# A four-layer graph attention kernel: groups of three row tiles in place of four, and a bias as three bf16 rows

## The chip, the cores and the metric

The kernel runs on one core of a Trainium2 chip. The metric is the device time of one execution in microseconds. The engines are named as in the profile: PE (TensorE, with PEld for its weight loads), DVE (VectorE), ACT (ScalarE), POOL (GpSimd) and SP, whose queue issues most DMAs.

## The reference

Four graph attention layers run over 4096 nodes with 256 features. Each ends in a residual sum and a layer norm. The adjacency matrix has density 1/256 plus the diagonal, about 17 neighbours a row, and all layers share it.

```python
# x (4096, 256) f32, adj (4096, 4096) int32
x = layernorm(x + L0(x, adj))     # 4 heads of 64: e = leaky(s_i + d_j, 0.2), masked softmax over j, times h
x = layernorm(x + L1(x, adj))     # 4 heads of 64, the same form
x = layernorm(x + L2(x, adj))     # 2 heads of 128, with biases b1, b2 (scores) and b3 (values)
x = layernorm(x + L3(x, adj))     # 1 head: softmax(e) @ x and -softmax(-e) @ x, joined, times fc_W, elu
```

## The kernel before

Rows are handled in 32 row tiles of 128 nodes. In `Program.run`, a layer is a sequence of row tiles (`Layer.steps`), each in two halves, and each row tile that is finished is projected for the next layer (`Projection`: transpose, two matmuls against the weights, factors, a store of the values row to DRAM).

There are two ways to compute a row tile. A *gathered* tile (`RowTile`) knows by a list which neighbours its rows have; the list is built during layer 0. It loads its own rows of values by a DMA on SP (L792) and the neighbours' by 13 indirect DMAs on POOL (L797), six for the first half and seven for the second. `RowTile.half` then forms the weights: ACT's Exp (L907; in layer 3 L874 to L877), DVE's mask (L864, L909, L876, L878), and PE multiplies weights and gathered values (L928). The units of a half are of two kinds: those of `FULL` use 128 columns of weights, those of `PAIRS` use 64 columns twice. The own rows are unit 0, the only one of `FULL[0]`.

An *all-node* tile is computed against all 4096 nodes instead. `WHOLE` lists, for each layer, blocks of four such row tiles (`BT = 4`); `ORDER` holds the rest, which are gathered. `whole_heads` does a block in layer 1 and `whole_rows` in layers 2 and 3. Both are generators: each `yield` ends one unit, the work of one block of 128 neighbours for all four row tiles of the block. A unit loads one `vw` tile of values (SP), spreads the bits of the adjacency to bytes (`bytes`, L660), forms the weights of 128 x 512 elements (DVE's L1275 in layer 1, with a product of exponentials and a maximum; ACT's L1200 or L1203 to L1207 and DVE's L1201 or L1208 in layers 2 and 3) and multiplies (PE: L1278 and L1280 in layer 1, L1211 in layers 2 and 3). A block has 64 units in layer 1 (two turns of two heads), 32 in layer 2 and 64 in layer 3 (two signs).

`half_with_whole` writes the order of a half step down: transposes of tiles to be projected, the half of the gathered tile, copies and matmuls of the projections, the end of the previous tile, then a share of the units. The share is set by `whole`:

```python
while self.between is None and self.used < self.total \
        and self.used < self.ahead + (self.total - self.ahead) * (step + 1) / (2 * self.count - 6):
    self.unit()
```

So the units are spread evenly over the half steps of the layer and end three tiles before it does. Ten units of the next layer (`AHEAD`) run at the change of layers, in `close`. A scheduler then places the instructions of each engine, so the final order can differ from the written one by a little.

The bias of layer 2 is added in `Projection.multiply`: a matmul of a column of ones with one row `brow` of 262 float32 numbers, after the two matmuls of the projection (L691, then L694). `weights(2)` builds that row.

`norm` collects finished rows and normalises them in groups; `GROUPS` gives the size of a group up to a tile number. `MIX = 23`: first halves gather only from tiles 0 to 22, second halves from all.

Of the kernel before, what the change touches and what calls it, by code (L numbers as in the profile page):

```python
# [81 lines left out]
GROUPS = (((24, 4),), ((24, 2), (28, 1), (31, 2)), ((16, 2), (17, 1), (20, 2), (24, 1), (31, 2)), ((24, 1), (31, 4)))  # L82
# [32 lines left out]
WHOLE = ((), (1, 7), (3, 7, 6), (7, 6))  # L115
AHEAD = 10
ORDER = tuple([m for m in range(NT) if m // BT not in w] for w in WHOLE)
# [66 lines left out]
class Program:  # L184
# [27 lines left out]
    def weights(self, n):  # L212
# [5 lines left out]
        if n < 2:  # L218
            nc.sync.dma_start(out=wext[:, :, :F], in_=to_tiles(ins[f"W{n}T"]))
            for k, a in enumerate(("src", "dst")):  # L220
                ablk = self.small.tile([P, KT, H4], F32, name=f"ablk{k}")
                nc.vector.memset(ablk, 0.0)
                for h in range(H4):
                    r = slice((h % 2) * D4, (h % 2) * D4 + D4)
                    vec = ins["a0s" if k == 0 else "a0d"][h] if n == 0 else ins["a1"][h, k * D4:(k + 1) * D4]
                    load_vec(nc, ablk[r, h // 2, h:h + 1], vec)
                ablks.append(ablk)
                nats.append(ins[f"W{n}"])
        elif n == 2:
            nc.sync.dma_start(out=wext[:, :, :F], in_=to_tiles(ins["W23T"]))  # L230
            for k in range(2):
                ablk = self.small.tile([P, KT, 2], F32, name=f"ablk{k}")
                nc.vector.memset(ablk, 0.0)
                for h in range(2):
                    load_vec(nc, ablk[:, h, h:h + 1], ins["a2"][h, k * P:(k + 1) * P])
                ablks.append(ablk)
                nats.append(ins["W21" if k == 0 else "W22"])
            brow = self.small.tile([1, F + 3 * H], F32, name="brow")
            nc.sync.dma_start(out=brow[:, :F], in_=ins["b23"].rearrange("(o f) -> o f", o=1))
            ones = self.small.tile([1, P], F32, name="ones")  # L240
            nc.vector.memset(ones, 1.0)
            self.ones = ones
        else:
            fc = to_tiles(ins["fc3"])
            for k in range(2):
                nc.sync.dma_start(out=wext[:, :, k * F:(k + 1) * F], in_=fc[:, k * KT:(k + 1) * KT, :])
                ablk = self.small.tile([P, KT, 1], F32, name=f"ablk{k}")
                for q in range(KT):
                    load_vec(nc, ablk[:, q, 0:1], ins["a3"][(k * KT + q) * P:(k * KT + q + 1) * P])
                ablks.append(ablk)  # L250
                nats.append(ins["W3T"])
# [29 lines left out]
        return wext, brow  # L281


    def lists(self, ctx):
# [94 lines left out]
        class Block:  # L379
# [21 lines left out]
            def squeeze(self, part):  # L401
# [10 lines left out]
                if part == BT - 1:  # L412
                    rows = shared["v"][0][self.blk % 2][:N, :BW].rearrange("(j p) w -> p j w", p=P)
                    nc.sync.dma_start(out=rows, in_=self.bits.rearrange("p j t w -> p j (t w)").bitcast(F32))
                    if any(self.blk in w for w in WHOLE):
                        nc.sync.dma_start(out=shared["bitsW"][self.blk], in_=self.bits)
# [189 lines left out]
    def run(self):  # L606
        ins, nc = self.ins, self.nc
        nothing = self.small.tile([1, max(PITCH)], F32, name="nothing")
# [148 lines left out]
class RowTile:  # L757
# [77 lines left out]
    def half(self, half):  # L835
# [82 lines left out]
        for t, heads in enumerate(turns):  # L918
            for us in (FULL[half], PAIRS[half])[::-1 if t == 1 and (half == 1 or n < 3) else 1]:
                for h in heads:  # L920
                    for u in us:
                        for rows, g in parts[u]:
                            a = accs[h][rows, :Wd] if n == 3 else accs[0][rows, h * Wd:(h + 1) * Wd]
                            b = g[:, h * Wd:(h + 1) * Wd]
                            if n < 2:
                                a = accs[0][rows, h * Wd:(H + 1) * Wd].rearrange("p (s c) -> p s c", c=Wd)[:, ::H - h]
                                b = b.rearrange("p (s c) -> p s c", s=1).to_broadcast([P, 2, Wd])
                            nc.tensor.matmul(a, w[h][:, u, rows], b,  # L928
                                             start=half == 0 and u == 0 and (n == 3 or h == turns[0][0]),
                                             stop=half == 1, skip_group_check=True)  # L930
# [24 lines left out]
class Layer:  # L955
# [3 lines left out]
    def __init__(self, prog, n):  # L959
# [6 lines left out]
        self.total = len(WHOLE[n]) * ((NT if n == 2 else 2 * NT) + (BT if n < 2 else 0))  # L966
# [201 lines left out]
    def whole_rows(self):  # L1168
# [3 lines left out]
        for blk in WHOLE[n]:  # L1172
            tiles = range(blk * BT, (blk + 1) * BT)
# [3 lines left out]
            bits = self.block_bits(blk)  # L1177
            zs = [None] * BT
            for heads in groups:
                accs = [prog.bank(prog.pfour) for _ in range(BT)]  # L1180
# [11 lines left out]
                for j in range(NT):  # L1192
# [3 lines left out]
                    for h in heads:  # L1196
                        p = prog.dp.tile([P, BT, P], F32, name="pw")
                        d = sh["d"][n][:, j, h if n < 3 else 0:h + 1 if n < 3 else 1]
                        if n < 3:
                            nc.scalar.activation(p, S[:, h], AF.Exp, bias=d)  # L1200
                            nc.vector.scalar_tensor_tensor(p, p, LEAST, mj, op0=ALU.max, op1=ALU.mult)  # L1201
                        else:
                            nc.scalar.activation(p, S[:, 0], AF.Relu, bias=d)  # L1203
# [6 lines left out]
                        for it in range(BT):  # L1210
# [3 lines left out]
                    if n == 3 and heads[0] == 0 and j == NT - 1:  # L1214
                        def between(accs=accs):
                            for it in range(BT):
                                zs[it], last = self.positive(accs[it], whole=True)
                            return last
# [8 lines left out]
    def whole_heads(self):  # L1227
# [8 lines left out]
        def scores(blk):  # L1236
            S = prog.bk.tile([P, T, BT, P], F32, name="Sw", bufs=2)
            for it in range(BT):
                nc.sync.dma_start(out=S[:, :, it, :], in_=sh["e"][n][blk * BT + it].partition_broadcast(P))
            return S  # L1240
# [11 lines left out]
        for q, blk in enumerate(WHOLE[n]):  # L1252
            tiles, S = range(blk * BT, (blk + 1) * BT), later
            bits = self.block_bits(blk)
            z = prog.bk.tile([P, BT, H, Wd], F32, name="zh")
            for up, flat in TWOS:
# [11 lines left out]
                for j in range(NT):  # L1268
# [4 lines left out]
                    for h in (up, flat):  # L1273
                        p[h] = prog.dp.tile([P, BT, P], F32, name="pw")
                        nc.vector.scalar_tensor_tensor(p[h], S[:, h], c[:, j, h:h + 1], mj, op0=ALU.max, op1=ALU.mult)  # L1275
                    how = dict(stop=j == NT - 1, skip_group_check=True)
                    for it in range(BT):
# [10 lines left out]
                nc.scalar.copy(z[:, :, up, :], bu[:, :BT * Wd].rearrange("p (t c) -> p t c", t=BT))  # L1288
                turned = prog.bk.tile([Wd, BT, P], F32, name="turned")
                nc.scalar.copy(turned, bf[:Wd, :].rearrange("p (t i) -> p t i", t=BT))  # L1290
                self.set_banks()
                bt = prog.bank(prog.banks)
                for it in range(BT):
                    nc.tensor.transpose(bt[:, it * Wd:(it + 1) * Wd], turned[:, it, :], sh["ident"][:Wd, :Wd])
                nc.scalar.copy(z[:, :, flat, :], bt[:, :BT * Wd].rearrange("p (t c) -> p t c", t=BT))
            y = self.load_x(tiles[0])
            for it, m in enumerate(tiles):
                yield
                self.finish(m, z[:, it].rearrange("p h c -> p (h c)"), y, None)
                if it + 1 < BT:  # L1300
                    y = self.load_x(m + 1)

    def block_bits(self, blk):
        bits = self.prog.mwp.tile([P, NT, BT, MW], I32, name="bw")
        self.nc.sync.dma_start(out=bits, in_=self.shared["bitsW"][blk])
        return bits

    def bytes(self, bits, j):
        mj = self.prog.mup.tile([P, BT, P // 4], I32, name="mw")
        spread(self.nc, mj, bits[:, j], self.shared["pat"])  # L1310
        return mj.rearrange("p t i -> p (t i)").bitcast(U8).rearrange("p (t i) -> p t i", t=BT)
# [548 lines left out]
```

## Time and profile before

| | us |
|---|---|
| median of 5 runs | 2786.59 |
| lowest and highest | 2770.5, 2790.01 |
| the profiled execution | 2783.01 |
| its span, first to last instruction | 2781.2 |
| mean granted TensorE clock | 0.834 |

| busy in the span | us | share | instructions |
|---|---|---|---|
| PE | 2126.6 | 76% | 15865 |
| DVE | 1597.4 | 57% | 5138 |
| ACT | 1553.4 | 56% | 4806 |
| POOL | 1319.3 | 47% | 1335 |

A matmul of float32 shows as two records. The busy time of a group is the union of its rows; the mean duration of one is longer than the distance between two starts, since matmuls overlap in the array. Layer 0, with the building of the lists, takes about the first 1100 us; layers 1, 2 and 3 take the rest in nearly equal parts. The DMA queues moved 454.91 MB.

### The profile page before, as it was taken

To read this page: it belongs to the slowest core of one execution; us is meant where nothing else is said; L and a number is where in the kernel's file an instruction comes from. 1 tells how busy PE (TensorE), PEld (TensorE's weight loads), DVE (VectorE), ACT (ScalarE), POOL (GpSimd) and SP (SyncE) were. 2 spreads that over 40 slices of the span, in tenths; PEclk is the share of its full clock that TensorE was granted. 3 is DMA by queue.
4 is the path that set the end of the run, shared out by engine and by line. 5 is a ranking of instruction groups with operands and counts; after the bars stand their busy time and mean duration, and the time that the engine had idled before them with its cause. 6 is when DMAs were issued, how large, how long until landed. Compare 5 with 4: busy or idle time off the path is not lost. (4 is left out here: it accounts for less than half of the span.)

```text
span 2781.2 us, 48223 instructions
## 1 busy us (share of the span) xinstructions
PE 2126.6 (76%) x15865; PEld 1714.2 (62%) x15865; DVE 1597.4 (57%) x5138; ACT 1553.4 (56%) x4806; POOL 1319.3 (47%) x1335
## 2 busy tenths in 40 slices
PE   5636766666667768588888887758899888999997
PEld 3335545544545556477777786647787766676675
DVE  3335535554553446466666776536777574667675
ACT  5436545554554345555555555546766656666674
POOL 0244443444444343644444453355666426666663
PEclk7657767776776779799989998868999899999998
DMA  8757555554543345444444443335556557778774
GB/s 276 252 184 231 165 159 169 160 169 156 169 150 99 91 142 145 114 122 130 124 131 126 131 137 112 107 98 146 161 166 165 136 162 217 232 238 250 240 237 142
DMA packets 299344, 454.91 MB, mean 164 GB/s; under 512 B 89830, under 2 KB 215371, under 8 KB 299084
## 3 DMA queue, kind: packets, MB, share of 16 engines
q0 software_dynamic: 72384, 220.69, 27.4%
q1 hardware_dynamic: 222082, 226.84, 27.3%
q10 hardware_dynamic: 4618, 4.20, 0.4%
q8 instruction: 128, 2.10, 0.3%
q14 instruction: 132, 1.08, 0.1%
HBM read 402.49 MB, written 49.08 MB: 162 GB/s over the span
## 5 line engine op out<-in xcount | busy, mean ns | idle before, releaser
L797 POOL DMA_INDIRECT G<-vals,idx x1300 | 1313.8, 1011 | 1432.5 <-issue 582.0
L928 PE MATMUL bank<-G,w 128*64 128x130 f32 (+5 forms) x8708 | 1089.6, 332 | 371.8 <-issue 333.6
L928 PEld LDWEIGHTS bank<-G,w 128*64 128x64 f32 (+1 forms) x8708 | 840.6, 175 | 598.2 <-issue 499.9
L907 ACT ACTIVATE w<-S,G 128x64 f32<-128x64 f32 (+1 forms) x3248 | 864.8, 351 | 191.4 <-PE bank L928 70.2
L1211 PE MATMUL bank<-vw,pw 128*128 128x129 f32 (+1 forms) x2560 | 439.5, 327 | 47.1 <-issue 38.7
L1211 PEld LDWEIGHTS bank<-vw,pw 128*128 128x128 f32 x2560 | 386.0, 198 | 96.3 <-issue 57.3
L864 DVE SCALAR_TENSOR_TENSOR w<-w,bank 128x1024 f32<-128x1024 f32 (+1 forms) x224 | 299.4, 1346 | 58.5 <-ACT w L907 39.0
L1275 DVE SCALAR_TENSOR_TENSOR pw<-Sw,cw,mw 128x512 f32<-128x512 f32 x256 | 185.1, 747 | 114.1 <-remote 62.9
L691 PE MATMUL bank<-wext,xT 128*128 128x268 f32 (+3 forms) x640 | 198.9, 446 | 28.1 <-ACT xT L682 15.0
L1200 ACT ACTIVATE pw<-Sw,d 128x512 f32<-128x512 f32 x192 | 135.1, 713 | 128.8 <-remote 86.1
L1280 PE MATMUL bank<-pw,vw 128*65 128x128 f32 x1024 | 198.1, 279 | 4.2 <-issue 4.2
L1201 DVE SCALAR_TENSOR_TENSOR pw<-pw,mw 128x512 f32<-128x512 f32 x192 | 130.3, 687 | 117.7 <-ACT pw L1200 78.9
L1278 PE MATMUL bank<-vw,pw 128*128 128x65 f32 x1024 | 175.4, 256 | 7.7 <-issue 6.0
L1278 PEld LDWEIGHTS bank<-vw,pw 128*128 128x128 f32 x1024 | 157.9, 196 | 15.0 <-issue 11.6
L691 PEld LDWEIGHTS bank<-wext,xT 128*128 128x128 f32 x640 | 129.2, 218 | 59.2 <-ACT xT L682 18.6
L742 ACT ACTIVATE erow<-bank,shift 4x128 f32<-4x128 f32 (+1 forms) x96 | 34.0, 354 | 208.1 <-PE bank L732 114.0
L874 ACT ACTIVATE w<-S,G 128x64 f32<-128x64 f32 (+1 forms) x329 | 105.3, 352 | 79.6 <-DMA G<-vals,idx 44.6
L399 ACT ACTIVATE mk<-raw 128x1024 uint8<-128x1024 int32 x128 | 129.2, 1049 | 22.2 <-DMA raw<-in_adjB_dram 12.8
L711 ACT ACTIVATE row<-bank 128x4 f32<-128x4 f32 (+1 forms) x128 | 21.5, 168 | 206.4 <-remote 109.4
L1208 DVE TENSOR_TENSOR pw<-pw,mw 128x512 f32<-128x512 f32 x128 | 87.8, 689 | 82.5 <-issue 27.4
L682 ACT COPY xT<-bank 128x256 f32<-128x256 f32 x128 | 45.9, 362 | 130.3 <-PE bank L677 67.3
L1203 ACT ACTIVATE pw<-Sw,d 128x512 f32<-128x512 f32 x128 | 90.0, 710 | 45.3 <-remote 20.4
(195 smaller groups left out, 2055.5 us busy)
## 6 DMA issues: line engine op xcount, KB each, us to landing
raw<-in_adjB_dram SPq DMA_DIRECT2D x128, 512.0 KB
G<-vals,idx POOLq DMA_INDIRECT x1300
vw<-vals SPq DMA_DIRECT2D x128, 130.0 KB
vw<-vals SPq DMA_DIRECT2D x128, 128.5 KB
S<-edge SPq DMA_DIRECT2D x56, 256.0 KB
vw<-vals SPq DMA_DIRECT2D x96, 129.0 KB
xp<-y SPq DMA_DIRECT2D x96, 128.0 KB
y<-xp SPq DMA_DIRECT2D x96, 128.0 KB
```

The lines of the kernel that those rows point to most:

```text
L399: nc.scalar.activation(self.mk[:, 2 * q:2 * q + 2], src, AF.Copy)
L691: nc.tensor.matmul(pp[:, :c1 - c0], self.xT[:, k, :], wext[:, k, c0:c1], start=(k == 0), stop=(k == KT - 1 and brow is None))
L797: nc.gpsimd.indirect_dma_start(out=self.row(half, k), out_offset=None, in_=self.values[:N + 1 if half else MIX * P, :].rearrange("r (k c) ...
L864: return nc.vector.scalar_tensor_tensor(pair, pair, LEAST, mh2, op0=ALU.max, op1=ALU.mult)
L907: nc.scalar.activation(w[h][:, u, rows], S[:, h, rows], AF.Exp, bias=d(g, h))
L928: nc.tensor.matmul(a, w[h][:, u, rows], b, start=half == 0 and u == 0 and (n == 3 or h == turns[0][0]), stop=half == 1, skip_group_check=True)
L1200: nc.scalar.activation(p, S[:, h], AF.Exp, bias=d)
L1201: nc.vector.scalar_tensor_tensor(p, p, LEAST, mj, op0=ALU.max, op1=ALU.mult)
L1211: nc.tensor.matmul(accs[it][:, c:c + Wd], p[:, it, :], v[:, c:c + Wd], start=(j == 0 and h == heads[0]), stop=(j == NT - 1), skip_group_ch ...
L1275: nc.vector.scalar_tensor_tensor(p[h], S[:, h], c[:, j, h:h + 1], mj, op0=ALU.max, op1=ALU.mult)
L1278: nc.tensor.matmul(bu[:, it * Wd:(it + 1) * Wd], p[up][:, it, :], v[:, up * Wd:(up + 1) * Wd], start=j == 0 and it == 0, **how)
L1280: nc.tensor.matmul(bf[:Wd, it * P:(it + 1) * P], v[:, flat * Wd:(flat + 1) * Wd], p[flat][:, it, :], start=j == 0 and it == 0, **how)
```

## The change

It has four parts.

- `WHOLE` now holds ranges of row tiles instead of block numbers. Layer 1 has tiles 5-7 and 29-31 where it had 4-7 and 28-31; layer 2 has 12-15, 28-31 and 25-27 where it had 24-27; layer 3 has 28-31 and 25-27 where it had 24-27. So two more row tiles are gathered in layer 1, one more in layer 2 and one more in layer 3, and the loops of `whole_heads` and `whole_rows` run over `g = len(tiles)`. The number of units is as before (128, 96 and 128); a unit of a group of three has weights of 128 x 384 and three quarters of the matmuls. `GROUPS` is moved by a tile to fit.
- In layer 3, the first half of a gathered tile multiplies its own rows for both signs before the neighbours' for both; before it did own and neighbours' rows of one sign, then those of the other.
- The bias row of layer 2 is split into three bf16 rows (`thirds`), each the rest of the one before, laid on three partitions by DMAs. The matmul that adds it is a bf16 one over three rows.
- The row of zeros that is stored after the values is taken from a gather slot instead of a tile of its own.

```diff
-GROUPS = (((24, 4),), ((24, 2), (28, 1), (31, 2)), ((16, 2), (17, 1), (20, 2), (24, 1), (31, 2)), ((24, 1), (31, 4)))
+GROUPS = (((24, 4),), ((24, 2), (29, 1), (31, 2)), ((16, 2), (17, 1), (20, 2), (25, 1), (31, 2)), ((25, 1), (28, 3), (31, 4)))
-WHOLE = ((), (1, 7), (3, 7, 6), (7, 6))
+WHOLE = (
+    (),
+    (range(5, 8), range(29, 32),),
+    (range(12, 16), range(28, 32), range(25, 28),),
+    (range(28, 32), range(25, 28),),
+)
-            ones = self.small.tile([1, P], F32, name="ones")
+            self.ones = self.small.tile([3, P], BF16, name="ones")
...
-        return wext, brow
+        return wext, None if brow is None else self.thirds(brow)
+
+    def thirds(self, row):
+        nc, width = self.nc, row.shape[1]
+        out = self.small.tile([3, width], BF16, name="thirds")
+        for k in range(3):
+            one = self.small.tile([1, width], BF16, name="third")
+            nc.vector.tensor_copy(one, row)
+            nc.sync.dma_start(out=out[k:k + 1, :], in_=one)
+            if k < 2:
+                nc.vector.tensor_tensor(row, row, one, op=ALU.subtract)
+        return out
...
-        nothing = self.small.tile([1, max(PITCH)], F32, name="nothing")
+        nothing = self.g1.tile([P, SLOT], F32, name="G")[:1, :max(PITCH)]
...
-        for t, heads in enumerate(turns):
-            for us in (FULL[half], PAIRS[half])[::-1 if t == 1 and (half == 1 or n < 3) else 1]:
+        runs = [(us, heads) for t, heads in enumerate(turns) for us in (FULL[half], PAIRS[half])[::-1 if t else 1]]
+        if n == 3 and half == 0:
+            runs = [(us, heads) for us in (FULL[0], PAIRS[0]) for heads in turns]
...
-        self.total = len(WHOLE[n]) * ((NT if n == 2 else 2 * NT) + (BT if n < 2 else 0))
+        self.total = len(WHOLE[n]) * NT * (1 if n == 2 else 2) + (sum(map(len, WHOLE[n])) if n < 2 else 0)
...
-        for blk in WHOLE[n]:
-            tiles = range(blk * BT, (blk + 1) * BT)
+        for tiles in WHOLE[n]:
+            g = len(tiles)
...
-                accs = [prog.bank(prog.pfour) for _ in range(BT)]
+                accs = [prog.bank(prog.pfour) for _ in range(g)]
...
-                        p = prog.dp.tile([P, BT, P], F32, name="pw")
+                        p = prog.dp.tile([P, BT, P], F32, name="pw")[:, :g]
...
-                        for it in range(BT):
+                        for it in range(g):
                             nc.tensor.matmul(accs[it][:, c:c + Wd], p[:, it, :], v[:, c:c + Wd],
```

## The prediction

> **What bounds the kernel now.** I read the page first, then sums by layer, then who waits for whom inside a layer, then the rows of PE themselves. On the page PE leads, and its granted clock and its share both rise in the second half, where the three changed layers lie.
>
> ```profile
> PE 2126.6 (76%) x15865; PEld 1714.2 (62%) x15865; DVE 1597.4 (57%) x5138; ACT 1553.4 (56%) x4806; POOL 1319.3 (47%) x1335
> PE   5636766666667768588888887758899888999997
> PEclk7657767776776779799989998868999899999998
> ```
>
> L1278 runs first at 1100.7 us, L1211 for layer 2 at 1774.7, L1203 for layer 3 at 2216.5. So I cut the span at 1098, 1700 and 2216 and took busy time by layer (columns: stretch, us, then PE, PEld, DVE, ACT, POOL, granted clock, DMA share, GB/s).
>
> ```profile
> 1098.00:1700.00 602.00, 498.86 (x4485) 440.83 (x4484) 392.68 (x1019) 328.84 (x1247) 285.80 (x282) 0.90 0.46 128
> 1700.00:2216.00 516.00, 409.76 (x3163) 355.34 (x3163) 321.68 (x1091) 313.94 (x943) 280.24 (x260) 0.86 0.49 138
> 2216.00:2781.00 565.00, 504.94 (x2709) 368.95 (x2703) 364.33 (x1370) 358.78 (x824) 319.78 (x313) 0.95 0.70 213
> ```
>
> PE is at 83%, 79% and 89%; no other engine passes 65%. The waits of 1150 to 1700 say the same: POOL waits for a slot to come free, ACT and DVE wait for PE's banks, and PE itself mostly for nothing that the profile shows.
>
> ```profile
> POOL G L797 <- ACT w L907: 103.4, 15, 9.2
> ACT w L907 <- PE bank L928: 60.7, 25, 9.2
> PE bank L928 <- issue: 54.1, 96, 1.1
> DVE pw L1275 <- PE bank L1278: 21.3, 12, 4.9
> ```
>
> So in these layers a microsecond of PE is nearly one of the span, and the change is priced in PE time.
>
> **All-node tiles against gathered tiles.** The page's mean of a matmul is its latency; what counts is the distance between starts. Layer 1, PE's timeline:
>
> ```profile
> 1301.94 5.90 PE L928 MATMUL bank<-G,w 128*128 128x130 f32 x56
> 1308.06 0.34 PE L1278 MATMUL bank<-vw,pw 128*128 128x65 f32 x2
> 1308.23 0.39 PE L1280 MATMUL bank<-pw,vw 128*65 128x128 f32 x2
> 1308.45 0.33 PE L1278 MATMUL bank<-vw,pw 128*128 128x65 f32 x2
> ```
>
> One all-node row tile costs 1308.45 - 1308.06 = 0.39 us in each unit (two records each of two lines); 2 turns x 32 units make 25 us a tile. A gathered tile is 112 records; its half of 56 takes 4.8 (the chain has such rows) to 5.9 us, so 9.6 to 11.8 a tile, I take 11. Two tiles move: 2 x (25 - 11) = 28 us less. Lower bound: with the group's idle time before L928 (55.4 + 25.5 us on about 20 tiles, 4 a tile) 2 x (25 - 15) = 20. Upper: busy time of L1278 and L1280 counted apart, 373.5 / 8 = 47 a tile, gives 2 x (47 - 11) = 72, but it counts their overlap twice, so I stay near the lower end. Layers 2 and 3, from the chain of waits:
>
> ```profile
> 2042.10 2.12 PE bank L928 x28
> 2044.21 5.36 PE bank L1211 x48
> ...
> 2419.54 4.68 PE bank L928 x28
> 2424.22 5.20 PE bank L1211 x24
> 2429.42 3.97 PE bank L928 x28
> 2433.38 5.40 PE bank L1211 x24
> ```
>
> In layer 3 these follow one another without a gap: that is a layer at PE's pace. An all-node tile is 128 records in each layer: layer 2, 5.36 / 48 x 128 = 14.3 us; layer 3, 5.20 / 24 x 128 = 27.7 us. A gathered tile is 56: about 5 us in layer 2 (halves of 2.1 to 2.6), 8.65 in layer 3. One tile moves in each: 9 and 19 us less. Sum of the three layers: 28 + 9 + 19 = 56.
>
> **What does not shrink, and what grows.** The number of units stays (128, 96, 128), and with it the loads of vw and the count of instructions on DVE and ACT; only their width goes from 512 to 384. DVE's L864 rows (1481 ns for 1280, 1214 for 1024) give 1.04 ns an element, so L1275 falls from 747 to about 614 ns. ACT's rows of 128 and 512 elements (388 and 710 ns) give about 600 for 384. Neither is on the path, so I book nothing. What four more gathered tiles add elsewhere: 13 gathers each on POOL, 1.25 us apart in its rows (0.95 and 0.30 idle), 16.3 us a tile; in layer 1 that is 26 x 16.3 = 423 us of some 550, 77% where it was 65%. ACT in layer 1 gets 112 more of L907 at 0.28 (328 us for 1160), 32 us, 361 in all; DVE loses 128 x 0.33 (two L1275 and L660) and gains about 16 (two tiles, each four L864 rows, 5.4 us, and the smaller ones), 367 in all. All still under PE's some 450. What hides them is PE's own pace; without that cover POOL would cost 4 x 16.3 = 65 us, which is the third rival below. On PE itself four tiles bring four times the idle time seen before L928 (4, 2.3, 1 us by layer; the first counts the disturbed start, so I take 2.5): 2 x 2.5 + 2.3 + 1 = 8 us more.
>
> **The bias.** Each tile projected for layer 2 pays L694 after its two matmuls:
>
> ```profile
> 1712.85 1.05 PE L691 MATMUL bank<-wext,xT 128*128 128x262 f32 x4
> 1713.83 0.70 PE L694 MATMUL bank<-brow,ones 1*128 1x262 f32 x2
> 1714.46 1.15 PE L691 MATMUL bank<-wext,xT 128*128 128x262 f32 x4
> ```
>
> From 1712.85 to 1714.46 is 1.61 us for four and two records; four at the 0.22 that lies between L691's starts are 0.88, so the bias costs 0.73. After it is one bf16 matmul in place of two records of float32. No bf16 matmul of this width is in the trace. Bounds: 0 saved if only the switch to one row and back counts, 0.73 if it vanishes. I take 0.30 left, one stream of 262 columns at half a record (0.11) and two switches of about 0.09 (below): 0.43 x 32 = 14 us, range 0 to 23. [...]
>
> The three rows have to be made: three copies, two subtractions of 262 elements on one partition, and three DMAs on SP, each waiting for DVE, with DVE's second copy waiting for the first DMA. They stand at the start of layer 1 (brow's last write is at 1087.4). DVE sits idle from 1088.6 to 1096.3 there, which hides the wait; the third DMA stands ahead of vw and S loads on SP, behind a copy that DVE reaches some 25 L1275 later. Bounds 0 and 10 us (a stretch of 10.6 us in which SP is blocked on its vw loads anyway); I take 3.
>
> **Own tiles first.** In first halves of layer 3 the order wide, narrow, wide, narrow becomes wide, wide, narrow, narrow: two changes of weight width fewer. PE's starts in layer 3 lie 310 ns apart (median) at such a change, 217 between wide ones: 0.09 x 2 x 25 = 5 us. It makes the narrow matmuls of one head wait for the mask of the other, which is long ready when PE is behind. The new G-slot source of the zero row and the new normalisation groups cost nothing: five small DMAs ahead of everything, and a few 0.15 us operations on DVE.
>
> **Sum.** 56 + 14 + 5 - 8 - 3 = 64 us. Not all reaches the end: in 1100-1150, 1700-1750 and 1800-1850, about a tenth of the three layers, PE is busy under 32 us of 50 and waits for gathers. I take nine tenths, 57. The profiled execution took 2783.0 us (span 2781.2), 3.6 below the median; 2783.0 - 57 = 2726 there, and 2786.6 - 57 = 2730 on the median.
>
> [...] The granted clock is 0.90 in layer 1, and 0.62 in 1800-1850 where PE is busy 21.75 of 50 us; within 1150-1700 the longest wait of PE is 4.9 us, once (L1294), the others under 2. [...]
>
> **Rivals.**
> 1. PE's idle share stays instead of its idle time, and the span of each layer shrinks with its PE work: 602 x 38/499 + 516 x 13/410 + 565 x 24/505 (bias and order included) = 89 us, 2698. For it: much idle before L928 comes with PE's own stream. Chance 0.10.
> 2. The row tile's step has its own pace (gather, Exp, mask, matmul), and units only fill it. A step is 25.1 us in layer 1 (602/24), 25.8 in layer 2, 23.5 in layer 3. Four more steps at these are 100 us, less 19 for bias and order: 2868. It decides once a step of layer 1 stays above 602/26 = 23.2 us; halfway it gives about 2800 to 2830. For it: PE rows one at a time at 1124-1143 while 26 gathers run in a row. Against it: the layer 3 chain above, and POOL at 16.3 us. Chance of slower 0.11.
> 3. POOL, or the DMA engines (0.75 to 0.85 busy in layer 3), take what PE gives: 65 us of gathers against 64 saved, no change. Against: POOL still waits for slots. Chance 0.09.
> 4. Half of the tile term is lost, as more gathers meet the same slow stretches, about 2755; part of the forecast's own range.
>
> Forecast with 4: 0.70. Faster by over 0.5% (about what a measurement here can tell; the five runs lie 0.7% apart): 0.80; within: 0.09; slower: 0.11. The range goes from 2692 (rival 1) to 2785 (rival 3 and part of 2). The likeliest case's own range is 2700 to 2765.
>
> **What would show it.** Right: layer 1 near 550 us, layer 3 near 540 with the same closed chain, L1211 rows of x18 where x24 stood in the second block; the bf16 bias near 0.3 us between L691 groups; first halves of layer 3 near 3.8 instead of 3.97. Wrong: layer 1's step still near 25 us with more idle before L928 or ACT's L907 waiting for gathers; DMA share of layer 3 above 0.85 with L1211 waiting for vw; PE silent after 1110 while SP stands at the third row's DMA.

## The result, and the profile after

The changed kernel took 2800.6 us (median of 24 runs, 2782.8 to 2814.9) and the kernel before 2783.3 (45 runs): ratio 1.0062, interval 1.0045 to 1.0078. It is 17 us slower where 57 less were forecast. One thing is needed to read all later numbers: the same kernel before took 2015 to 2017 us in four batches of runs and 2723, 2777 and 2783 in three others, one chip showed both, and all kernels of a batch share its level; so kernels are compared inside a batch only, and I call the two the short and the long level. The recorded comparison is of the long one.

The page after, the lines that answer to those of before (busy time, then tenths of PE and of the granted clock in 40 slices):

```profile
PE 2098.6 (75%) x15397; PEld 1681.3 (60%) x15397; DVE 1561.3 (56%) x5213; ACT 1576.4 (56%) x4964; POOL 1365.2 (49%) x1387
...
PE   5537766666667667588878788857888879998886
...
PEclk7656767777777778689889898969999989998998
```

PE lost 468 matmuls and 28 us of busy time, as the change says, and its share fell all the same. By layer, cut where the next layer's first unit runs, as before (stretch, us, PE, PEld, DVE, ACT, POOL, granted clock, DMA share, GB/s):

```profile
1105.00:1707.00 602.00, 470.71 (x4099) 410.25 (x4098) 353.79 (x1011) 344.72 (x1327) 306.48 (x305) 0.86 0.47 132
1707.00:2228.00 521.00, 410.12 (x3140) 353.62 (x3135) 326.45 (x1162) 324.12 (x1005) 290.06 (x276) 0.88 0.52 144
2228.00:2807.70 579.70, 495.60 (x2616) 361.88 (x2616) 356.46 (x1367) 354.91 (x836) 333.55 (x326) 0.92 0.70 213
```

Layer 1 takes 602 us as it did before, with 28 us less of PE busy time in it; layer 2 takes 5 more and layer 3 15 more. The idle time has grown in the place where the prediction had said to look. The waits of 1155 to 1700 (total, times, longest):

```profile
PEld bank L946 <- issue: 116.9, 189, 1.3
...
PE bank L946 <- issue: 81.9, 120, 1.2
...
DVE pw L1293 <- PE bank L1296: 30.2, 14, 6.2
```

L946 was L928. PE's idle time ahead of it rose from 54.1 to 81.9 us, in pieces of at most 1.2 us that no semaphore explains. One such patch of layer 1, PE's timeline and POOL's:

```profile
1355.73 1.27 PE L946 MATMUL bank<-G,w 128*64 128x130 f32 x14
1357.42 0.44 PE L946 MATMUL bank<-G,w 128*64 128x130 f32 x3 [0.42 <-issue]
1358.18 0.48 PE L946 MATMUL bank<-G,w 128*64 128x130 f32 x4 [0.32 <-issue]
1358.95 0.42 PE L946 MATMUL bank<-G,w 128*64 128x130 f32 x2 [0.28 <-issue]
1359.67 0.27 PE L946 MATMUL bank<-G,w 128*64 128x130 f32 x1 [0.30 <-issue]
1360.42 0.30 PE L946 MATMUL bank<-G,w 128*64 128x130 f32 x1 [0.48 <-issue]
1361.82 2.41 PE L946 MATMUL bank<-G,w 128*64 128x130 f32 x15 [1.10 <-issue]
```

```profile
1356.09 0.95 POOL L813 DMA_INDIRECT G<-vals,idx  x1 [0.30 <-issue]
1357.34 0.95 POOL L813 DMA_INDIRECT G<-vals,idx  x1 [0.30 <-issue]
1358.59 0.94 POOL L813 DMA_INDIRECT G<-vals,idx  x1 [0.30 <-issue]
1359.84 1.19 POOL L813 DMA_INDIRECT G<-vals,idx  x1 [0.30 <-issue]
```

While POOL issues gathers at its 1.25 us pace, PE gets a handful of matmuls about every 0.75 us, and the profile shows no semaphore that it waits for. I call this the crawl. POOL's run ends at 1361.0; from 1361.8 PE runs 15 in 2.4 us again.

The trace of before has such patches too, so the prediction had them in front of it. PE's pauses of over 0.3 us that no semaphore explains, added up from its rows in layers 1 to 3 (layers cut as in the next section), are 100.5, 63.1 and 36.7 us before and 133.9, 67.9 and 57.5 after: 200 in all, then 259. In layer 1, 36 of the 42 runs of gathers (gathers less than 0.5 us apart) have one before and 41 of 47 after. As such runs cover over half of the layer, their place alone proves little; the runs without gathers below do.

### The profile page after: what moved, and what is told of

It is laid out like the page before. It is cut to its first block, busy times and chain, and to the rows that moved or that the text cites. A ratio compares the mean times of both kernels' runs of the same rounds, so it can differ in the third digit from the quotient of the medians.

```text
span 2807.7 us, 47611 instructions
## 1 busy us (share of the span) xinstructions
PE 2098.6 (75%) x15397; PEld 1681.3 (60%) x15397; DVE 1561.3 (56%) x5213; ACT 1576.4 (56%) x4964; POOL 1365.2 (49%) x1387
## 5 line engine op out<-in xcount | busy, mean ns | idle before, releaser
L813 POOL DMA_INDIRECT G<-vals,idx x1352 | 1359.9, 1006 | 1410.4 <-issue 595.5
L946 PE MATMUL bank<-G,w 128*64 128x130 f32 (+5 forms) x9044 | 1141.5, 332 | 366.1 <-issue 330.5
L946 PEld LDWEIGHTS bank<-G,w 128*64 128x64 f32 (+1 forms) x9044 | 884.5, 175 | 592.0 <-issue 491.3
L923 ACT ACTIVATE w<-S,G 128x64 f32<-128x64 f32 (+1 forms) x3388 | 901.1, 350 | 147.4 <-remote 53.4
L1229 PEld LDWEIGHTS bank<-vw,pw 128*128 128x128 f32 x2304 | 354.6, 202 | 135.3 <-issue 99.6
L1293 DVE SCALAR_TENSOR_TENSOR pw<-Sw,cw,mw 128x384 f32<-128x384 f32 x256 | 151.2, 612 | 101.1 <-remote 36.2
L1218 ACT ACTIVATE pw<-Sw,d 128x512 f32<-128x512 f32 (+1 forms) x192 | 127.6, 678 | 112.6 <-PE bank L1229 44.1
L1219 DVE SCALAR_TENSOR_TENSOR pw<-pw,mw 128x512 f32<-128x512 f32 (+1 forms) x192 | 121.6, 643 | 101.7 <-ACT pw L1218 71.4
L707 PEld LDWEIGHTS bank<-wext,xT 128*128 128x128 f32 x640 | 130.8, 221 | 67.9 <-ACT xT L698 24.6
L1298 PE MATMUL bank<-pw,vw 128*65 128x128 f32 x768 | 155.3, 289 | 18.4 <-issue 18.4
L890 ACT ACTIVATE w<-S,G 128x64 f32<-128x64 f32 (+1 forms) x343 | 112.0, 354 | 95.5 <-DMA G<-vals,idx 57.8
L1296 PEld LDWEIGHTS bank<-vw,pw 128*128 128x128 f32 x768 | 126.8, 209 | 26.9 <-issue 24.3
L1226 DVE TENSOR_TENSOR pw<-pw,mw 128x512 f32<-128x512 f32 (+1 forms) x128 | 79.1, 622 | 79.3 <-ACT pw L1223 29.8
```

Source lines behind the costliest of these rows:

```text
L707: nc.tensor.matmul(pp[:, :c1 - c0], self.xT[:, k, :], wext[:, k, c0:c1], start=(k == 0), stop=(k == KT - 1 and brow is None))
L813: nc.gpsimd.indirect_dma_start(out=self.row(half, k), out_offset=None, in_=self.values[:N + 1 if half else MIX * P, :].rearrange("r (k c) ...
L923: nc.scalar.activation(w[h][:, u, rows], S[:, h, rows], AF.Exp, bias=d(g, h))
L946: nc.tensor.matmul(a, w[h][:, u, rows], b, start=half == 0 and u == 0 and (n == 3 or h == turns[0][0]), stop=half == 1, skip_group_check=True)
L1218: nc.scalar.activation(p, S[:, h, :g], AF.Exp, bias=d)
L1229: nc.tensor.matmul(accs[it][:, c:c + Wd], p[:, it, :], v[:, c:c + Wd], start=(j == 0 and h == heads[0]), stop=(j == NT - 1), skip_group_ch ...
```

## The experiments

The cut in this section is at the last narrow transpose (L732 before, L748 after) that a layer's projections make, since every kernel has it; against the cut above it moves some 87 us from layer 2 to layer 1 and some 55 from layer 3 to layer 2. The recorded pair by this cut, before and then after:

```profile
1098.00:1787.00 689.00, 563.27 (x5004) 491.65 (x5002) 442.37 (x1230) 382.67 (x1443) 308.56 (x306) 0.89 0.44 125
1787.00:2270.00 483.00, 396.19 (x3002) 346.20 (x3003) 315.19 (x1087) 290.22 (x830) 257.82 (x237) 0.89 0.51 143
2270.00:2781.00 511.00, 454.10 (x2344) 327.27 (x2342) 321.12 (x1164) 328.67 (x738) 319.44 (x313) 0.94 0.73 222
```

```profile
1100.00:1794.00 694.00, 544.30 (x4680) 468.53 (x4678) 411.99 (x1261) 405.07 (x1544) 332.05 (x332) 0.87 0.46 130
1794.00:2284.00 490.00, 389.49 (x2931) 338.94 (x2932) 312.83 (x1107) 296.03 (x878) 276.94 (x258) 0.89 0.53 149
2284.00:2808.00 524.00, 447.63 (x2272) 322.44 (x2270) 316.87 (x1185) 323.31 (x748) 321.11 (x318) 0.91 0.73 220
```

PE's busy time in the three layers falls by 32 us (1413.6 to 1381.4), its idle time grows by 57 (269.4 to 326.6), and the pauses without a semaphore grow by 59, as much as all of it.

The table has layer times in us from sums by stretch of the profiled run, and medians against the kernel before of the same batch. The kernel before has no profile at the short level; its layers there are read from kernels that leave the layer as it was (491, 382 and 470).

| kernel | level | layer 0 | 1 | 2 | 3 | median against before |
|---|---|---|---|---|---|---|
| before | long | 1098 | 689 | 483 | 511 | 2783.3 |
| after | long | 1100 | 694 | 490 | 524 | 1.0062 [1.0045, 1.0078] |
| all but layer 2's groups | long | 1091 | 699 | 477 | 531 | 1.0078 [1.0044, 1.0112] |
| bias and order alone | long | 1064 | 676 | 475 | 511 | 1.0006 [0.9975, 1.0037] |
| before, more gathers | long | 1108 | 826 | 577 | 654 | 1.1410 [1.1351, 1.1470] |
| after, more gathers | long | 1100 | 842 | 595 | 650 | 1.1536 [1.1477, 1.1595] |
| before, plain transfers | long | 1040 | 482 | 352 | 448 | 0.8573 [0.8523, 0.8624] |
| after, plain transfers | long | 1045 | 441 | 333 | 421 | 0.8244 [0.8192, 0.8295] |
| layer 1's groups alone | short | 676 | 461 | 382 | 470 | 0.9883 [0.9869, 0.9898] |
| layer 2 and 3's groups alone | short | 680 | 491 | 391 | 458 | 1.0019 [1.0008, 1.0030] |
| bias and order alone | short | 674 | 488 | 378 | 464 | 0.9951 [0.9938, 0.9964] |
| matmuls left out | short | 671 | 470 | 378 | 461 | 0.9826 [0.9810, 0.9842] |
| after | short | 672 | 455 | 400 | 458 | 0.9879 [0.9862, 0.9897] |
| all but layer 2 and 3's groups | short | 677 | 457 | 387 | 465 | 0.9859 [0.9844, 0.9874] |
| before, plain transfers | short | 676 | 482 | 351 | 446 | 0.9708 [0.9692, 0.9724] |
| after, plain transfers | short | 677 | 444 | 332 | 424 | 0.9339 [0.9314, 0.9363] |
| after, four tiles plain | short | 674 | 454 | 395 | 453 | 0.9812 [0.9786, 0.9839] |
| twelve tiles over all nodes | short | 676 | 574 | 405 | 467 | 1.0532 [1.0504, 1.0559] |

**The parts one by one.** Each starts from the kernel before; the edits are told in short.

```diff
 # layer 1's groups alone
-GROUPS[1] = ((24, 2), (28, 1), (31, 2));  WHOLE[1] = blocks 1, 7
+GROUPS[1] = ((24, 2), (29, 1), (31, 2));  WHOLE[1] = (range(5, 8), range(29, 32))
 # layer 2 and 3's groups alone
+GROUPS[2], WHOLE[2], GROUPS[3], WHOLE[3] of the change
 # bias and order alone: thirds(), the bf16 ones, `nothing` from a G slot, own tiles first
 # matmuls left out
+FEWER = ((), (1, 7), (6,), (6,))
+def mine(n, blk, j):
+    return range(BT - 1) if blk in FEWER[n] and j not in (0, blk * BT + BT - 1, NT - 1) else range(BT)
...
-                        for it in range(BT):
+                        for it in mine(n, blk, j):
```

> The kernel before with layer 1's groups alone (5-7 and 29-31). By the prediction's sum (PE sets the pace): 28 - 5 = 23 us less, ratio 0.992. Rival A, gathers in a row slow PE and ACT and halve PE's clock, so that a gathered tile costs more than its matmuls: the layer grows from 590 to 602 us between the two traces, so 8 to 15 us more, ratio 1.003 to 1.005.

> The kernel before with the groups of three of layers 2 and 3 alone. By the prediction's sum: 9 + 19 - 3 = 25 us less, ratio 0.991. Rival A: the traces show layer 2 shorter by 5 and layer 3 longer by 14 us, so about 9 more, ratio 1.003.

> The bias as three bf16 rows and the own tiles first, with the blocks of before. By the prediction's sum: 14 + 5 - 3 = 16 us less, ratio 0.994. Rival A says nothing of these two; if the whole change costs 17 us because of the groups, this stays at 10 to 16 less. Rival C, the wait for the three rows at the start of layer 1 costs what the matmuls save: no change, ratio 0.998 to 1.002.

> The kernel before, without adding a gathered tile: in both blocks of layer 1, the third of layer 2 and the second of layer 3 the fourth row tile's matmuls are left out in 29 of 32 units of each turn (so these rows are wrong). Only PE's work falls, by 45 us in layer 1, 13 in layer 2, 25 in layer 3, 83 in all at the starts' distances. Prediction's theory: nine tenths of it, 75 us less, ratio 0.973. Rival B, the row tile's step has its own pace and units fill it: under 25 us less, ratio above 0.991. Rival A alone: between, 40 to 75 less, since PE is freed but the slow stretches at the gathers stay.

Measured, all at the short level (before 2015.7): 24 less, 5 more, 9 less, 35 less. There PE is busy for 95% to 98% of layer 1 in these four, and the layer's term came out; the sums by stretch of layer 1's groups alone and then of layer 2 and 3's groups alone, one row each of layers 1 and 2:

```profile
676.00:1137.00 461.00, 450.57 (x4712) 406.69 (x4712) 413.71 (x1261) 403.70 (x1548) 341.73 (x335) 0.99 0.71 198
1137.00:1519.00 382.00, 353.95 (x3003) 323.38 (x3003) 312.93 (x1091) 291.21 (x838) 263.31 (x237) 0.97 0.64 181
```

```profile
680.00:1171.00 491.00, 481.82 (x5005) 440.92 (x5004) 437.82 (x1230) 379.03 (x1443) 321.36 (x307) 0.99 0.64 177
1171.00:1562.00 391.00, 347.71 (x2928) 315.92 (x2926) 306.45 (x1097) 291.25 (x863) 277.86 (x258) 0.95 0.66 186
```

Layer 1 fell from 491 to 461. In layer 2 PE's busy time fell by 6 while the layer grew from 382 to 391: PE is at 93% without the groups, 89% with them. Leaving out matmuls worth 83 us at the distances of their starts, and nothing else, brought 35. (The 75 of the two expectations below is nine tenths of these 83.) PE's busy time by the sums fell by 65 us: 35, 10 and 20 by layer, against the same layers of the other parts. So even here only about half of PE's time is the span's. The gain came from layer 1 (491 to 470) and layer 3 (470 to 461), and hardly from layer 2 (382 to 378). The same kernel brought 35 in two later batches, also at this level (ratios 0.9838 and 0.9814); how much it brings at the long level is open:

> The kernel before with the fourth tile's matmuls left out in the two blocks of layer 1 and in block 6 of layers 2 and 3, in 29 of 32 units, as in the earlier run of it (those tiles' sums lack these nodes): 75 us of PE's time and nothing else. Where the kernel before takes 2015 us it brought 35. Where it takes 2720 to 2780: 10 to 35 less by theory 4, since PE's work lies beside gathers that hold the engines up anyway; 60 to 75 less if PE's busy time sets the pace there as the prediction had it.

> The same left-out matmuls once more, for a run in which the kernel before takes 2720 to 2780 us: 10 to 35 less by theory 4, 60 to 75 less if PE's busy time sets the pace there. Where it takes 2015, 35 less a third time.

**The whole change at this level, and the gathers as plain transfers.**

```diff
 # RowTile.load, in the loop over k
+            if n > 0:
+                q = pos % MIX
+                nc.gpsimd.dma_start(out=self.row(half, k), in_=self.values[q * P:(q + 1) * P, :ROW[n]])
+                continue
             nc.gpsimd.indirect_dma_start(
```

> The whole change, on one chip beside the kernel before. Theory 1 (the parts add): 24 us less for layer 1's groups, 5 more for layers 2 and 3's, 9 less for the rest: 28 less, ratio 0.986. Theory 2 (the parts work against one another, and that is the recorded loss): the recorded ratio of 1.006 comes back. Theory 3 (what the recorded traces show, PE and ACT down to one instruction in 0.7 us while POOL issues gathers, belongs to the surroundings of that run and not to the change): ratio 0.986 where the layers' gather patches run without that crawl, 1.006 where it is there; the trace says which of the two this run was.

> Layer 1's groups of three, the bias and the own tiles first; layers 2 and 3 keep their blocks of four. If the parts add: 24 + 9 = 33 us less than before and 5 less than the whole change, ratio 0.984. If layers 2 and 3's groups only looked dear without the rest: no faster than the whole change.

> The kernel before, with each gather of layers 1 to 3 (12 in a row tile) as one plain transfer of the same bytes on POOL's queue (other rows than the reference's). [...] Theory POOL (gathers set the pace of layers 2 and 3, 520 us for layer 3 against 469 to 487 of PE): layer 3 falls to PE's busy time and a tenth, 500 or less, layer 2 by 10 to 20 us, layer 1, where PE is busy 96%, by under 10. Theory PE (or the row tiles' own chain) : all three layers within 10 us of before.

> The changed kernel, with the same plain transfers (other rows than the reference's). Against the kernel before with them: theory POOL gives the groups of layers 2 and 3 back the 20 to 25 us of PE's time that the prediction counted, 45 to 60 us less in all; theory PE (or chain) gives the same difference as with the gathers, 28 us less or, if the recorded one is the true one, 17 more.

The whole change took 1989.4 against 2015.3: the sign is the other one here, and the parts add (28 expected, 26 measured). Without layers 2 and 3's groups it took 1987.9; adding the parts gave 33 less than before, 27 were measured, and the 1.5 us between the two kernels are within their spread. The gather patches have no crawl: PE has no pause of over 0.3 us without a semaphore in any layer of this trace. PE's timeline and POOL's of the changed kernel at the short level:

```profile
799.84 0.39 PE L1298 MATMUL bank<-pw,vw 128*65 128x128 f32 x2
800.06 4.07 PE L946 MATMUL bank<-G,w 128*128 128x130 f32 x56
803.97 0.22 PE L1296 MATMUL bank<-vw,pw 128*128 128x65 f32 x1
```

```profile
799.07 0.95 POOL L813 DMA_INDIRECT G<-vals,idx  x1 [0.30 <-issue]
800.32 1.33 POOL L813 DMA_INDIRECT G<-vals,idx  x1 [0.30 <-issue]
801.95 0.95 POOL L813 DMA_INDIRECT G<-vals,idx  x1 [0.30 <-issue]
803.20 0.95 POOL L813 DMA_INDIRECT G<-vals,idx  x1 [0.30 <-ACT w L923]
```

POOL does the same at the same pace, and PE does 56 matmuls in 4.07 us beside it. All 13 gathers of a row tile are replaced in the two kernels with plain transfers, not 12 as the expectation has it. The plain ones read rows of tiles 0 to 12 alone, so a second half no longer waits for the last tiles of the layer before; what that brings is part of what follows and was not separated. With plain transfers the kernel before fell by 58 us and the changed one by 110: without gathers the change is worth 77.6 us (1957.2 to 1879.6). So the gathers take 52 us of the change's worth here. Theory POOL had the direction; its 45 to 60 for the change with plain transfers was too little. Of the theories on the change itself, 1 and 3 hold: the parts add, and the crawl belongs to the surroundings of a run, as this one has neither the crawl nor the loss.

**More gathers.** Two indirect DMAs more in each half of layers 1 to 3, into columns that nobody reads.

```diff
+        for k in (HALF - 2, HALF - 1) if n > 0 else ():
+            pos = half * HALF + k - 1
+            slot = self.slot(half, (HALF - 1) // PER[n])
+            c = (HALF - 1) % PER[n] * ROW[n] + ROW[n] + 92 * (k - HALF + 2)
+            nc.gpsimd.indirect_dma_start(
+                out=slot[:, c:c + 92], out_offset=None, ...
```

> The kernel before with four more gathers in each row tile of layers 1 to 3 (13 become 17; two in each half, 92 columns wide, that nobody reads). Theory POOL: a gather takes its turn of 1.25 us on POOL, a row tile then can't take less than 17 x 1.25 = 21.3 us: layer 1 with 24 row tiles 510 us (488 without the extra gathers), layer 2 with 20 row tiles 425 (378), layer 3 with 24 row tiles 510 (464); some 115 us more in all. Theory PE: PE does nothing more, so under 30 us more.

> The changed kernel with the same four more gathers. Theory POOL: the change adds four row tiles, 4 x 21.3 = 85 us of gathers, so that it is slower than the kernel before with them by 40 to 85 us, where without them it was 25 us faster: the sign turns over, as in the recorded comparison. Theory PE: still some 25 us faster than the other.

> The change without its part in layer 2 (whose blocks stay (3, 7, 6), 20 row tiles). If layer 2's pace is its row tiles' (378 us for 20, 400 for 21), 13 to 20 us less than the whole change: 1969 to 1976 us, ratio 0.977 to 0.980. If layer 2's loss came from elsewhere: 1985 to 1992.

This batch ran at the long level (before 2776.5). 272 more gathers in the kernel before brought 388 us, 1.43 us each, over three times what theory POOL had said. POOL's groups and the sums by stretch of that kernel:

```profile
L797 POOL DMA_INDIRECT G<-vals,idx x1300 | 1308.1, 1006 | 1469.3 <-issue 572.8 <-ACT w L914 276.5 <-DVE idx L528 112.4
L804 POOL DMA_INDIRECT G<-vals,idx x272 | 266.6, 980 | 82.9 <-issue 82.6 <-DMA G<-vals,idx 0.3
```

```profile
1108.00:1934.00 826.00, 631.20 (x5002) 533.44 (x5002) 444.13 (x1228) 385.24 (x1444) 399.86 (x400) 0.82 0.40 110
```

POOL is busy under half of layer 1 (399.9 of 826 us) and still waits for ACT to free slots, so it isn't POOL's own time that sets the pace. What the kernel loses for a gather, 1.43 us, is near what a gather takes on POOL (0.98 busy and 0.30 after it). PE shows 631 us busy for work that takes 480 without gathers. The change with the extra gathers was 31 us slower than before with them, under the 40 to 85 that theory POOL had. Without its part in layer 2 the change is slower too (1.0078), with 10 us more in layer 1 and 20 in layer 3 than the profile of before has; so at this level the loss does not belong to layer 2. As the whole change was not in this batch, the two can't be compared.

**Plain transfers at the long level.** The same two kernels as above, and bias and order alone.

> The kernel before with plain transfers for the gathers of layers 1 to 3 (other rows than the reference's), as in the earlier run of it, now for a chip on which the kernel before takes 2777 us. There 272 more gathers cost 388 us, 1.43 us each, although a gather keeps POOL alone busy 1.0 us. Theory 4 (there a gather holds up the other engines for about as long as POOL works on it): without the 884 gathers of layers 1 to 3 those layers fall from 1683 us to about what they took with plain transfers on the other chips, 1279; with layer 0's 1100 that makes about 2380. Theory 5 (that chip is slower throughout): ratio 0.97 as there, about 2695. If this run falls on a chip of the other kind, 1957 again.

> The changed kernel with the same plain transfers. Theory 4: 1199 us in layers 1 to 3 as on the other chips, 2300 in all, 80 less than the kernel before with them: the sign of the recorded comparison turns over. Theory 5: slower than the kernel before with them, by the recorded half per cent. On a chip of the other kind, 1880 again.

> Bias thirds and own tiles first alone, with the old blocks of four: no gather more or fewer than before. Theory 4: it gains here too what it took from PE, 9 us as on the other chips to the 16 predicted: 2761 to 2768, ratio 0.994 to 0.997, and is then the one version that is faster than before on both kinds of chip. Theory 5: within 5 us of before.

Before took 2723.5 in this batch, 2337.3 with plain transfers, and the changed kernel with them 2245.7. The sums by stretch of layers 1 to 3, the kernel before and then the changed one, both with plain transfers:

```profile
1040.00:1522.00 482.00, 479.36 (x5004) 437.89 (x5003) 435.28 (x1230) 380.14 (x1451) 162.58 (x306) 1.00 0.61 180
1522.00:1874.00 352.00, 342.24 (x3001) 316.06 (x3002) 308.64 (x1084) 294.37 (x858) 124.64 (x234) 0.99 0.71 206
1874.00:2322.00 448.00, 431.09 (x2345) 320.30 (x2344) 317.65 (x1166) 313.43 (x703) 152.82 (x287) 0.99 0.73 237
```

```profile
1045.00:1486.00 441.00, 435.40 (x4680) 398.04 (x4680) 403.75 (x1262) 402.25 (x1542) 175.91 (x332) 1.00 0.69 205
1486.00:1819.00 333.00, 327.98 (x2930) 303.74 (x2931) 305.74 (x1107) 298.84 (x906) 131.01 (x247) 0.99 0.76 224
1819.00:2240.00 421.00, 401.88 (x2273) 304.41 (x2272) 310.48 (x1187) 304.64 (x721) 159.59 (x300) 0.98 0.80 262
```

POOL's group of the plain transfers, in the kernel before:

```profile
L799 POOL DMA_DIRECT2D G<-vals x884 | 470.0, 539 | 840.1 <-issue 249.2 <-ACT w L911 234.1 <-PE bank L932 229.2
```

This settles that layers 1 to 3 are longer at the long level only with their gathers. In the kernel before with plain transfers they take 482, 352 and 448 us here and 482, 351 and 446 at the short level: without gathers the two levels are one. Layer 0, which keeps its gathers, stays at 1040. The pauses tell the same: in the kernel before with plain transfers PE has 240 us of pauses over 0.3 us without a semaphore in layer 0 and none in layers 1 to 3. The wait for the last tiles, which the plain transfers drop too, ends by a semaphore and so is none of these pauses; at the short level it and all else that they drop came to 58 us. PE is busy for 95% to 99% of these layers and its clock is granted almost in full. Theory 4 stands (2380 and 2300 expected), theory 5 falls. The change is worth 92 us here, where it cost 17 with its gathers in the recorded batch: they take 109 us of its worth. By the sums of layers 1 to 3 the change is 87 us less without gathers, all of it PE's busy time, and 25 more with them: PE's busy time falls by 32 in place of 87, and its idle time grows by 57 in place of none. The added gathers alone would be 52 x 1.43 = 74 of the 109, an estimate from the gathers that nobody reads; the rest would be PE's time that is saved beside the gathers that stay, and lost there. Bias and order alone brought nothing at this level (1.0006), against 9 us at the short one.

**The other way round, and four tiles plain.**

```diff
 # twelve tiles: bias and order alone, and
-    (range(4, 8), range(28, 32),),
+    (range(4, 8), range(28, 32), range(24, 28),),        # GROUPS[1] = ((16, 2), (24, 1), (31, 2))
 # four tiles: the changed kernel, plain transfers where
+            if m in ((), (4, 28), (24,), (24,))[n]:
```

> The other way round: bias thirds and own tiles first with the old blocks, and in layer 1 a third block of four (tiles 24 to 27) over all nodes, so that 20 row tiles are gathered there in place of 24, 52 gathers fewer. Where the kernel before takes 2015 us, layer 1 is PE's (482 us at 97% busy), and four tiles cost 4 x 20 us more there: some 2075 to 2085, ratio 1.03 or more. Where it takes 2720 to 2780 theory 4 has the change's loss turned over: 17 us less or more than that, ratio 0.980 to 0.995; a theory in which only PE's work counts has ratio 1.02 or more there too.

> The changed kernel, with plain transfers for the four row tiles alone that the change adds (4 and 28 in layer 1, 24 in layers 2 and 3; other rows than the reference's in these four), so that it issues the 1300 gathers of the kernel before. Where the kernel before takes 2015 us (the whole change: 25 less): 13 to 20 us of layer 2 and some of layer 3 come back, 45 to 55 less than before in all, ratio 0.973 to 0.978. Where it takes 2720 to 2780 (the whole change: 17 more): with 1.43 us for each of 52 gathers 57 less, ratio 0.98; if the added gathers are not what costs there, 0 to 17 more.

Both fell on the short level. Twelve all-node tiles in layer 1 in place of eight cost 108 us against the kernel before, where 60 to 70 were expected. Against bias and order alone (another batch) it is 117: 86 in layer 1 (574 for 488, 21.5 a tile against 20 expected), 27 in layer 2 and 3 in layer 3. Layer 2's 27 were not expected and stay unexplained. Whether fewer gathered tiles win at the long level was not measured. With plain transfers in the four added tiles the change brought 38 us where it had brought 26, not 45 to 55: layer 2 stayed at 395. So of the 52 us that gathers take from the change at the short level, the added ones are some 12; the rest goes with the 1300 that stay, and how was not tested. At the long level these four tiles were not run. Of the kernels that gather the reference's rows, no version was shown to be faster than the kernel before at both levels: bias and order alone, the only part run at both, gains 9 us at the short one and nothing at the long one.

## Why the prediction was wrong

**The step that failed** is the cover. The prediction said of the four tiles' gathers that "what hides them is PE's own pace", booked nothing, and priced the loss of that cover at 65 us. The cover is not there at this level: with the gathers made plain, the change is worth 92 us; with them it loses 17. The term that was put at nothing is 109 us (92 and 17 are of two batches), more than the whole forecast, and turns its sign. The price of 65 was too low as well, because it counted POOL's time only (1.25 us a gather), while PE is held up beside most runs of gathers (36 of 42 in layer 1 of before), those that were there before too.

**The reading behind it.** "A microsecond of PE is nearly one of the span" was read from busy shares of 79% to 89%. Those contain the stretches in which PE is granted half its clock (43 in layers 1 to 3 of before, 316 us in all) and its crawl. Layer 1 of before shows 563 us busy (by the second cut) for matmuls that take 479 without gathers, and when the change takes some of them away, PE's idle time grows by more than its busy time falls (57 against 32 us in layers 1 to 3). The closed chain that stood for layer 3 covers 19 of its 565 us, and PE is idle for 60 of them. Bias and order show it without any gather added: 16 us expected from PE, nothing measured (interval from 7 less to 10 more). The nine tenths of the sum should have been far less. The rows that hinted at it were in the prediction: PE one at a time at 1124 to 1143 while 26 gathers ran in a row, used for rival 2 and set aside on POOL's 16.3 us a tile.

**The rivals.** Rival 2, that a row tile's step keeps its pace, named 23.2 us in layer 1 as the point from which it decides and 2800 to 2830 halfway. The step is 602 / 26 = 23.2, in layer 3 23.2 where it was 23.5, and the time 2800.6. It had 0.11. That the number came out is partly luck, as layer 2's step did not stay (24.8 where it was 25.8) and layer 1's fell from 25.1. Its mechanism is the nearest of the three; what it lacked is that what holds the step goes with the gathers: with plain transfers PE is busy for 99% of layer 1. The range's lower end of 2692 is called rival 1's, whose sum is 2698.

**Terms that held, measured without gathers.** Layer 1 with bias, its window: 28 + 14 - 5 - 3 = 34 predicted, 41 and 38 measured at the long and the short level. Layer 2: 9 - 2 = 7, measured 19. Layer 3: 19 + 5 - 1 = 23, measured 27 and 22. The tile terms were right or low. A gathered half of 56 matmuls takes 4.07 us in the patch shown at the short level, where the prediction took 4.8 to 5.9 from rows of the long one. The bias, from PE's timeline of the changed kernel:

```profile
1720.19 1.05 PE L707 MATMUL bank<-wext,xT 128*128 128x262 f32 x4
1721.17 0.28 PE L710 MATMUL bank<-thirds,ones 3*128 3x262 bf16 x1
1721.38 0.44 PE L693 MATMUL bank<-ident,y 128*128 128x128 f32 x2
```

From 1720.19 to 1721.38 is 1.19 us; less four records at 0.22, the bias has 0.31 left (0.30 predicted). The 0.11 that the prediction counts in it for the stream of 262 columns was the author's estimate: no run shows it by itself, and these rows give the 0.31 as a whole. DVE's unit is as predicted (612 ns, about 614 predicted), and DVE still waits for PE's banks:

```profile
L1293 DVE SCALAR_TENSOR_TENSOR pw<-Sw,cw,mw 128x384 f32<-128x384 f32 x256 | 151.2, 612 | 101.1 <-remote 36.2 <-PE bank L1296 32.4 <-issue 17.7
```

**The clock** has no term in the sum: the waits of PE from 1150 to 1700 were under 2 us, but for one of 4.9, and that such waits cost no clock was the author's estimate, which the traces do not show. With gathers the changed kernel has 0.87, 0.89 and 0.91 in layers 1 to 3 (0.89, 0.89 and 0.94 before), with plain transfers 1.00, 0.99 and 0.98. From 1155 to 1700 of the changed kernel the granted clock falls to half 23 times, for 3.4 to 10.2 us each; before 21 of these falls no pause of PE in the last 8 us is over 1.2 us (before the other two the longest are 3.0 and 7.9). In the 3.4 us ahead of each fall, as long as the shortest of them lasts, PE's pauses add up to 1.35 us or more; so before the 21 there was more than one pause, each of at most 1.2 us. How much of the 109 us is clock was not separated.

**What stays open.** Why a batch falls on one level or the other, and what PE waits for in a patch. Not the packets: before and plain move the same 454.91 MB in the same 299344 packets, and packets of the gather queue take 169 ns at the long level and 165 at the short one (the changed kernel). Whether POOL's own work on a gather or something that goes with it holds the engines up, no run here tells. Nor was layer 0 run without gathers: that its 360 to 440 us more at the long level are theirs too is argued from its pauses.

## What to carry to other kernels

Before a saving on the busiest engine is priced as time, look at its pauses that no semaphore explains and at what another engine does in them: if they lie inside runs of indirect DMAs, as here, where an added gather cost 1.43 us at the long level, count gathers, not busy time. A change that trades matmuls for gathered tiles has two prices, that of its matmuls and that of its gathers; a pair of kernels with the gathers made plain, beside the pair with them, tells the two apart. Compare such changes at every level that the kernel shows: the same edit is 1.2% faster at one and 0.6% slower at the other.

## What the runs showed of the hardware

- The same program runs at 2015 to 2017 us or at 2723 to 2783; in the changed kernel the clock of PE is 0.937 or 0.821. Layers 1 to 3 without gathers take 1279 or 1282 us, so there the gathers make the difference; layer 0 with its 416 gathers takes 671 to 680 or 1040 to 1108.
- At the long level PE pauses beside gathers with no semaphore that the profile shows: with plain transfers 240 us of such pauses over 0.3 us in layer 0, which keeps its gathers, and none in layers 1 to 3; at the short level none in any layer of the changed kernel.
- In 545 us of the changed kernel at the long level the granted clock fell to half 23 times, for 3.4 to 10.2 us each, 21 times with no pause of PE over 1.2 us in the 8 us before; PE's pauses in the 3.4 us ahead of a fall add up to 1.35 us or more each time.
- At the long level an unused gather more costs 1.43 us of the whole kernel's time, though POOL is busy with it for 0.98 and is itself busy for half of the span.
- A plain transfer of the same bytes from POOL's queue keeps POOL for 0.54 us in place of 1.0, and PE beside it does not slow down (busy for 479 of the 482 us of layer 1, at a clock of 1.00).
